# Cross-attention values straight from block-transposed probabilities, on sixteen 32x32 tiles

## The chip, the core and the metric

The kernel runs on one core of a Trainium2 chip. The metric is the time in microseconds of one execution on the device, lower is better. A core has five engines with instruction queues of their own that meet only at semaphores: TensorE (PE in the profile, its weight loads PEld), VectorE (DVE), ScalarE (ACT), GpSimd (POOL) and SyncE (SP), which here only issues DMAs. SBUF and PSUM have 128 partitions; PSUM has eight banks.

## The reference

```python
# x: (32, 512, 640) f32, ctx: (32, 77, 1024) f32; 20 heads of 32
q = heads(x @ to_q_w)
k, v = heads(ctx[:, :77] @ to_k_w), heads(ctx[:, :77] @ to_v_w)
s = einsum('bhqd,bhkd->bhqk', q, k) / sqrt(32)
h_txt = einsum('bhqk,bhkd->bhqd', softmax(s), v)
# the object, others and ip branches read ctx[:, 77:], which has no rows, and add nothing
out = merge(h_txt) @ to_out_w + to_out_b + x
```

Arithmetic is of fp32 accuracy.

## The kernel before

The program is one list of instructions per engine, in the order in which the Python code emits them (a manual schedule); what follows is therefore also the order in which each engine works.

**Keys and values of the context, once.** All 32 x 77 context rows are multiplied with the key and value weights in groups of 512 rows. Both results go to DRAM: `k_dram` with 128 channels on partitions, `v_dram` with a row for each context row. To keep fp32 accuracy, an operand of a large product is split into a high and a low part (type fp32r), and a product is three matmuls, high x high, high x low and low x high (`PAIRS`). A matmul on plain fp32 operands (scores and values) appears in the trace as two records, each with its own weight load.

**Slots.** The rest is 160 slots, `slot(n)`, with n = 5b + j: batch b (512 rows of x), and j one of five groups of four heads (128 channels). `HPC` is 4 heads, `NQ` 4 blocks of 128 query rows, `NC_` 5. A slot emits, for TensorE:

- `scores(n)`: 16 matmuls, 4 query blocks by 4 heads. Each uses one strip of 32 rows of the array (a head has 32 channels), so four heads go to four strips, with 128 query columns as weights and 77 keys as moving data. The four heads have a PSUM bank each (tag `sc`).
- `values(n - 3)`: 4 matmuls, one per head, over 80 rows (77 keys and padding, `KPAD`) and 512 query columns, on four strips of 32 columns. Result `pa`, one bank.
- `piece(b, i)`: part of the output projection of an earlier batch (`po`, `project`), two pieces per slot, 24 matmuls together. `STEPS` and `CUTS` say which.
- `queries(n + 1)`: 15 matmuls, the queries of the next slot (`pq`).

Beside it: `maxima(n)` on VectorE (negative row maxima of the scores), `exps(n, i)` on ScalarE (16 exponentials with row sums, head by head), `sums` and `normalize` (a reciprocal on VectorE, a multiplication on GpSimd, into `pn`, 80 columns per head), `high_a` and `low_a` (the split of `pa`, ScalarE copy and VectorE subtraction), `copy_q` (`pq` to `qt`), `transpose_x` and `split_x` (the x of the next batch, transposed by 32x32 blocks on VectorE, split on ScalarE and GpSimd), `add_bias` on GpSimd, and `finish`, which adds residual and bias to a finished half row block and sends the output.

**The way through DRAM.** The probabilities have queries on partitions, the values need keys there. `transpose_p(n - 1)` transposes 32x32 blocks on VectorE into `z`: partition 32a + i of a block of 32 keys then holds key i for the 128 queries of four runs of 32 rows (one run from each query block). The four partition groups a thus hold the same keys for different queries. Four DMAs per slot write this to `pd` in DRAM so that rows are keys, and `load_p` reads it back one to two slots later as `raw`, 80 keys by 4 heads by 512 queries. With these hops, `LAG` is 3: the values of slot n - 3 stand behind the scores of slot n. Padding columns of `pn` are zero, so what stands in the padding rows of the value tile counts for nothing.

The first slots only fill the pipeline, with no projection in them (`filling`), and the last context values are computed in slots 0 and 1 (`beside`). `end()` works off the last values and the last batch's projection.

Of the kernel before, what the change touches and what calls it, by code (L numbers as in the profile page):

```python
# [29 lines left out]
KPAD = 80  # L30
NBLK = HPC * KPAD // Q

# [5 lines left out]
def kernel(  # L38
# [185 lines left out]
    def load_x(b, quarters=range(4)):  # L224

        if b not in xss:
            xss[b] = xpool[0].tile([P, S // Q, C // 4], F32, tag="xs", name="xs")
# [9 lines left out]
    def split_x(b, c, high=nc.scalar.copy, low=nc.gpsimd):  # L237

        xt = xpool[0].tile([P, 2, S], FPR, tag="xt", name="xt", bufs=7)
# [12 lines left out]
    for _ in range(12):  # L252
        nc.tensor.matmul(warm, zero[:, :P], zero, start=True, stop=True)
# [110 lines left out]
    main = ctx.enter_context(tc.tile_pool(name="main", bufs=1, reuse_waits="tile"))  # L364
    ps = ctx.enter_context(tc.tile_pool(name="ps", bufs=1, space=PSUM, reuse_waits="tile"))
    psv = tc.alloc_tile_pool(name="psv", bufs=3, space=PSUM, side="right", reuse_waits="tile")
    late = []

    raws, ats, pds, sms, pqs, pas, xrs, pos, scs, nms, rss = ({} for _ in range(11))
# [4 lines left out]
    vbs = [main.tile([KPAD, NC_, HPC, HD], F32, name=f"vb{n}") for n in range(2)]  # L374
# [6 lines left out]
    z = main.tile([P, NBLK, NQ, Q], F32, name="z")  # L381
# [3 lines left out]
    def load_values(b):  # L385
        nc.sync.dma_start(vbs[b % 2], v_dram[b * NKEY : b * NKEY + KPAD])

# [16 lines left out]
    def scores(n):  # L404
        b, j = divmod(n, NC_)
        scs[n] = [ps.tile([P, NQ, P], F32, tag="sc", name="sc", bufs=4) for _ in range(HPC)]
# [33 lines left out]
    def sums(n):  # L440
        rss[n] = main.tile([P, NQ * HPC], F32, tag="rs", name="rs", bufs=2)
        nc.vector.reciprocal(rss[n], sms.pop(n))  # L442

    def normalize(n):
        rs = rss.pop(n)
        pf = pnb[n % 2][:, :, :NKEY]
        nc.gpsimd.tensor_tensor(  # L447
            pf, pf, rs.unsqueeze(2).to_broadcast([P, NQ * HPC, NKEY]), ALU.mult
        )

    def transpose_p(n):

        pn = pnb[n % 2]
# [4 lines left out]
        pd = dram.tile([NBLK * Q, S], F32, tag="pd", name="pd", bufs=6)  # L458
        rows = pd.rearrange("(b i) q -> i b q", i=Q)
        for a in range(4):  # L460
            nc.sync.dma_start(  # L461
                rows[:, :, a * P : (a + 1) * P],
                z[a * Q : (a + 1) * Q].rearrange("p b t j -> p b (t j)"),
            )
        pds[n] = pd

    def load_p(n):
        pd = pds.pop(n)
        raw = late[0].tile([KPAD, HPC, S], F32, tag="raw", name="raw", bufs=2)
        nc.sync.dma_start(raw, pd.rearrange("(h k) q -> k h q", h=HPC))  # L470
        raws[n] = raw

    def values(n):
        b, j = divmod(n, NC_)
        raw, vb = raws.pop(n), vbs[b % 2][:, j]
        pas[n] = late[1].tile([P, S], F32, tag="pa", name="pa", bufs=1)
        for i in range(HPC):
            nc.tensor.matmul(  # L478
                pas[n][i * HD : (i + 1) * HD, :],
                vb[:, i, :],  # L480
                raw[:, i, :],
                start=True,
                stop=True,
                tile_position=(0, i * HD),
            )

    def high_a(n):
        if n >= N - NC_ + 1:
            at = xpool[0].tile([P, 2, S], FPR, tag="xt", name="at", bufs=7)
        else:  # L490
            at = late[0].tile([P, 2, S], FPR, tag="at", name="at", bufs=8)
        nc.scalar.copy(at[:, 0, :], pas[n])  # L492
        ats[n] = at

    def low_a(n):
        at = ats[n]
        nc.vector.tensor_tensor(  # L497
            at[:, 1, :], pas.pop(n), at[:, 0, :].bitcast(F32), ALU.subtract
        )

    def load_residual(b, t, xr=None):
        if xr is None:
            xr = late[0].tile([P, C], F32, tag="xr", name="xr", bufs=4)
# [21 lines left out]
    STEPS = [(0, h, j) for h in range(2) for j in range(4)] + [(0, 0, 4), (0, 1, 4)]  # L525
    STEPS += [(t, h, j) for t in range(1, NQ) for h in range(2) for j in range(NC_)]
    CUTS = (0, 4, 8, 10, 16, 20, 24, 28, 32, 36, 40)
# [25 lines left out]
    LAG = 3  # L553

    takes = {n + LAG: n for n in range(N)}

    PIECES = {2: (1, 0), 3: (1, 2), 4: (1, 4), 0: (2, 6), 1: (2, 8)}
    RESIDUAL = {1: (1, 0), 2: (1, 1), 3: (1, 2), 4: (1, 3)}  # L560
    BIAS = {2: (1, 0), 3: (1, 1), 4: (1, 2), 0: (2, 3)}
    TRANSPOSE_X = {0: ((0,), (1,)), 1: ((2,), (3,))}
    SPLIT_X = {2: (0, 1), 3: (2, 3, 4)}
# [3 lines left out]

    def take(m):
        values(m)
        high_a(m)  # L570
        low_a(m)

    def slot(n, beside=()):
# [4 lines left out]
        xsplits = SPLIT_X.get(j, ()) if more and n > LATE else ()  # L578
        turns = TRANSPOSE_X.get(j, ((), ())) if more and b else ((), ())
        if b == 1 and j < 2:  # L580
            turns = (((), ()), ((0, 1), (2, 3)))[j]
        taken = takes.get(n)
        filling = not has_out
# [11 lines left out]
        if j == 1:  # L595
            load_values(b)
        if n == NC_:
            load_x(b + 1, (2, 3))
        if j == 4 and b and b + 2 < B:
            load_x(b + 2, (0, 1))  # L600
# [4 lines left out]
        if has_out:  # L605
            piece(bo_, first)
        for i in range(2):
            exps(n, i)
        if n:
            transpose_p(n - 1)  # L610
        finish()
        if j == 4 and b + 2 < B:
            load_x(b + 2, (0, 1) if not b else (2, 3))
        for i in turns[0]:
# [7 lines left out]
        if filling and ahead:  # L622
            copy_q(n + 1, nc.vector.tensor_copy)
        for i in range(2, HPC):
            exps(n, i)
        sums(n)
# [5 lines left out]
        if has_out:  # L632
            piece(bo_, first + 1)
        if taken is not None:
            low_a(taken)
        for c in xsplits:
            split_x(b + 1, c)
        for i in turns[1]:
            transpose_x(b + 1, i)
        finish()  # L640

    def end():
# [3 lines left out]
        load_p(N - 2)  # L646
        add_bias(last - 1, 3)
        piece(last - 1, 6)
        finish()
        transpose_p(N - 1)  # L650
        load_p(N - 1)
        load_residual(last, 0)
        load_residual(last, 1)
        piece(last - 1, 7)
        finish()
        take(N - 3)
# [3 lines left out]
        load_residual(last, 2)  # L660

        def begin(i, j0, j1):
            t, h = divmod(i, 2)
            if j0 == 0:
                if i < 4:
                    pos[last, t, h] = ps.tile([P, S], F32, tag="sc", name="po", bufs=4)
                elif i == 4:
                    pos[last, t, h] = ps.tile([P, S], F32, tag="pq", name="po", bufs=1)
# [100 lines left out]
```

## Time and profile before

| | us |
|---|---|
| median of 3 runs | 1806.47 (1802.81 to 1807.61) |
| the profiled execution, its own time | 1809.79 |
| its span (first to last instruction) | 1808.0 |
| slot 0 begins (scores) | 264.61 |
| slot 8, the first of the steady ones, begins | 345.17 |
| slot 159, the last, begins | 1770.00 |

Mean granted TensorE clock 0.987 of full speed. The DMA engines move 389 MB, 215 GB/s on average, and are busy for 0.91 of the steady part.

How to read the rows that follow. A row of the timeline has the start in the span, the length from the first start to the last end (us), engine, line, operation, output <- inputs, shapes and a count; in brackets, how long the engine had been idle and what ended that. `32*128` behind the names of a TensorE row is the part of the array in use, rows by columns. Rows of costly groups have busy time and mean ns of one, then idle time before them. Rows of one line's instructions have a count and the shortest, median and longest duration in ns. The rows of a stretch have its length, each engine's busy time with instruction counts, the granted clock, the DMA engines' busy share and GB/s. Rows of waits have total us, times, longest. Durations of matmuls and loads include pipeline latency: they overlap, so what counts is from start to start.

### The profile page before, as it was taken

The numbers are of one execution on the slowest core, as the hardware profiler recorded it, in microseconds if no ns is written. First come the engines' busy times: TensorE is split into PE (matmuls) and PEld (weight loads), VectorE is DVE, ScalarE is ACT, GpSimd is POOL, SyncE is SP. The second block draws the span as 40 slices with busy tenths as digits, with TensorE's granted clock in tenths as the row PEclk, the third lists the DMA queues.
The fourth block names the chain that finished last, engine by engine and source line by source line (L and its number), as shares of the span: only waits on it lengthen the run. The fifth ranks groups of instructions, "written<-read, shape, count | busy, mean of one in ns | idle before, by whom it ended". The sixth has DMA issues, their size and how long they took to land.

```text
span 1808.0 us, 39341 instructions
## 1 busy us (share of the span) xinstructions
PE 1763.3 (98%) x13852; PEld 1440.0 (80%) x13852; DVE 933.3 (52%) x1651; ACT 1108.9 (61%) x5698; POOL 789.7 (44%) x502
## 2 busy tenths in 40 slices
PE   8999998899999999999999999999999999999999
PEld 7888896678878888877788777888788888877787
DVE  5233134555555555555555555555555555545553
ACT  3132035666767777767677776677676777666662
POOL 0000034444445555545555545545555555535453
PEclk9999999999999999999999999999999999999999
DMA  9746465899999999998999999998899999898987
GB/s 186 149 94 174 105 168 138 211 231 235 232 232 239 232 243 235 240 235 219 237 232 237 228 230 237 230 233 230 229 234 230 229 240 237 229 224 219 236 207 202
DMA packets 465173, 389.12 MB, mean 215 GB/s; under 512 B 91280, under 2 KB 372368, under 8 KB 464976
## 3 DMA queue, kind: packets, MB, share of 16 engines
q1 hardware_dynamic: 462384, 379.49, 84.5%
q0 software_dynamic: 2496, 6.97, 1.3%
q8 instruction: 109, 1.79, 0.4%
q14 instruction: 88, 0.72, 0.1%
q10 hardware_dynamic: 96, 0.16, 0.0%
HBM read 223.82 MB, written 162.70 MB: 214 GB/s over the span
## 4 chain that ended last, share of the span: by engine, by line
PE 63%; DMA 17%; ACT 6%; POOL 6%; SPq 4%; DVE 2%; issue 2%; POOLq 0%; DVEq 0%; ACTq 0%
PE po L515 20%; PE pq L393 17%; PE pk L177 7%; PE pv L177 7%; DMA raw<-pd 6%; DMA pd<-z 6%; ACT pn L432 6%; PE sc L410 5%; PE pa L478 5%; POOL xt L243 4%; DMA xs<-in_x_dram 4%; SPq L461 2%; POOL pn L447 1%; SPq L231 1%; DVE xs L235 1%
## 5 line engine op out<-in xcount | busy, mean ns | idle before, releaser
L432 ACT ACTIVATE pn<-sc,nm 128x77 f32<-128x77 f32 x2560 | 787.4, 361 | 400.2 <-DVE nm L422 379.6
L515 PEld LDWEIGHTS po<-wo_s,at 128*128 128x128 f32 x3840 | 582.7, 190 | 143.8 <-issue 132.1
L447 POOL TENSOR_TENSOR pn<-pn,rs 128x1232 f32<-128x1232 f32 x160 | 364.0, 2275 | 665.1 <-DVE rs L442 659.9
L515 PE MATMUL po<-wo_s,at 128*128 128x320 f32 x3840 | 636.8, 316 | 0.0
L432 ACT ACTIVATION_READ_ACCUMULATOR pn<-sc,nm 128x1 f32 x2560 | 618.7, 242 | 0.0
L393 PE MATMUL pq<-xt,wq_s 128*128 128x512 f32 x2400 | 582.8, 395 | 0.0
L393 PEld LDWEIGHTS pq<-xt,wq_s 128*128 128x128 f32 x2400 | 450.1, 190 | 92.8 <-issue 4.9
L422 DVE TENSOR_REDUCE nm<-sc 128x4 f32<-128x308 f32 x640 | 261.0, 469 | 202.2 <-PE sc L410 202.1
L454 DVE STREAM_TRANSPOSE z<-pn 128x1280 f32<-128x1280 f32 x160 | 241.1, 1507 | 97.8 <-DMA pd<-z 92.3
L508 POOL TENSOR_TENSOR xr<-xr,bias 128x640 f32<-128x640 f32 x128 | 200.8, 1569 | 94.2 <-DMA xr<-in_x_dram 85.9
L243 POOL TENSOR_TENSOR xt<-xs,xt 128x512 fp32r<-128x512 f32 x160 | 200.0, 1274 | 35.6 <-ACT xt L242 35.6
L478 PE MATMUL pa<-raw,vb 80*32 80x512 f32 x1280 | 173.4, 613 | 27.6 <-DMA raw<-pd 19.6
L410 PEld LDWEIGHTS sc<-kb,qt 32*128 32x128 f32 x5120 | 157.5, 186 | 41.0 <-issue 35.1
L410 PE MATMUL sc<-kb,qt 32*128 32x77 f32 x5120 | 181.0, 277 | 8.7 <-DVE rs L442 5.8
L544 DVE TENSOR_TENSOR xr<-po,xr 128x320 f32<-128x320 f32 x256 | 117.5, 469 | 79.4 <-PE po L515 75.7
L235 DVE STREAM_TRANSPOSE xs<-xs 128x640 f32<-128x640 f32 x128 | 105.8, 832 | 74.2 <-DMA xs<-in_x_dram 74.2
L442 DVE RECIPROCAL rs<-sm 128x16 f32<-128x16 f32 x160 | 38.8, 243 | 196.3 <-ACT pn L432 196.3
L177 PE MATMUL pk<-ct,wk_s 128*128 128x512 f32 (+1 forms) x600 | 136.0, 387 | 3.1 <-ACT wk_s L89 3.1
L402 ACT COPY qt<-pq 128x512 f32<-128x512 f32 x153 | 93.3, 610 | 72.5 <-PE pq L393 72.1
L177 PE MATMUL pv<-ct,wv_s 128*128 128x512 f32 (+1 forms) x600 | 133.9, 381 | 0.0
L177 PEld LDWEIGHTS pk<-ct,wk_s 128*128 128x128 f32 x600 | 114.2, 191 | 23.2 <-ACT wk_s L89 3.6
L497 DVE TENSOR_TENSOR at<-pa,at 128x512 fp32r<-128x512 f32 x160 | 108.6, 679 | 37.2 <-ACT at L492 37.1
(31 smaller groups left out, 536.7 us busy)
## 6 DMA issues: line engine op xcount, KB each, us to landing
pd<-z SPq DMA_DIRECT2D x640, 160.0 KB, 5.4
raw<-pd SPq DMA_DIRECT2D x160, 640.0 KB, 5.5
xs<-in_x_dram SPq DMA_DIRECT2D x128, 320.0 KB, 6.0
xr<-in_x_dram SPq DMA_DIRECT2D x128, 320.0 KB, 5.7
out_dram<-xr SPq DMA_DIRECT2D x127, 320.0 KB, 3.9
vb<-v_dram SPq DMA_DIRECT2D x32, 200.0 KB, 6.0
kb<-k_dram SPq DMA_DIRECT2D x32, 192.5 KB, 7.3
cs<-in_ctx_dram SPq DMA_DIRECT2D x12, 512.0 KB, 9.4
```

Of the source, the lines that this page charges most:

```text
L177: nc.tensor.matmul(held[j][:, :gn], w[:, k, a, :], cts[g, k][:, c, :gn], start=(k == 0 and n == 0), stop=(k == NK - 1 and n == 2),)
L235: nc.vector.transpose(part, part)
L243: low.tensor_tensor(parts[1], src, parts[0].bitcast(F32), ALU.subtract)
L393: nc.tensor.matmul(pqs[n], wq_s[:, k, a, j * P : (j + 1) * P], xts[b, k][:, c, :], start=(k == 0 and m == 0), stop=(k == NC_ - 1 and m == 2),)
L410: nc.tensor.matmul(sc[:, t, :NKEY], qts[n % 2][r, t * P : (t + 1) * P], kbs[b % 2][r, j, :], start=True, stop=True, tile_position=(i * HD, 0),
L422: nc.vector.tensor_reduce(nms[n][:, i], sc[:, :, :NKEY], AX.X, ALU.max, negate=True)
L432: nc.scalar.activation(pnb[n % 2][:, at, :NKEY], sc[:, t, :NKEY], AF.Exp, bias=nms[n][:, i, t : t + 1], accum_out=sms[n][:, at : at + 1],)
L447: nc.gpsimd.tensor_tensor(pf, pf, rs.unsqueeze(2).to_broadcast([P, NQ * HPC, NKEY]), ALU.mult)
L454: nc.vector.transpose(z.rearrange("p b t j -> p t b j"), pn.rearrange("p (t h) k -> p t (h k)", t=NQ).rearrange("p t (b i) -> p t b i", i=Q),)
L478: nc.tensor.matmul(pas[n][i * HD : (i + 1) * HD, :], vb[:, i, :], raw[:, i, :], start=True, stop=True, tile_position=(0, i * HD),)
L508: nc.gpsimd.tensor_tensor(xrs[b, t], xrs[b, t], bias, ALU.add)
L515: nc.tensor.matmul(pos[b, t, h][:, :HALF], ats[b * NC_ + j][:, a, t * P : (t + 1) * P], wos[0][:, j, c, h * HALF : (h + 1) * HALF], start= ...
```

## The change

The values take `z` directly as moving data. The partition groups a and the four heads i give sixteen tiles of 32 rows by 32 columns. For each block of 32 keys (`KBLK` = 3, keys padded to 96) sixteen matmuls of 128 columns follow on sixteen different tiles; the three blocks accumulate in PSUM, one bank per a. `pd`, `raw` and their DMAs go; the value tile `vb` is loaded four times, once per partition group. The values of slot n - 1 now stand late in slot n, behind the queries and the first piece, and use banks of the scores' tag, which has five and not four. `z` and `vb` are doubled (the second copies live in a pool that opens after slot 1).

Beside this: the evacuation works on four banks (four copies, four subtractions), the reciprocal moves into `normalize`, `transpose_p(n - 1)` stands directly behind the maxima, all exponentials stand together, the first piece of a slot has 2 steps (of three matmuls) and the second 6, projections of a batch begin at j = 1, x is double buffered and loaded by quarters, residual tiles are 3, and 22 matmuls on zeros warm the array at the start where there were 12.

```diff
-KPAD = 80
+KPAD = 96
 NBLK = HPC * KPAD // Q
+KBLK = KPAD // Q
...
-    for _ in range(12):
+    for _ in range(22):
         nc.tensor.matmul(warm, zero[:, :P], zero, start=True, stop=True)
...
-    def load_values(b):
-        nc.sync.dma_start(vbs[b % 2], v_dram[b * NKEY : b * NKEY + KPAD])
+    def load_values(b, parts=range(4)):
+        src = v_dram[b * NKEY : b * NKEY + KPAD].rearrange("(c i) j h d -> i c (j h d)", i=Q)
+        for a in parts:
+            dst = vbs[b % 2][a * Q : (a + 1) * Q].rearrange("i c j h d -> i c (j h d)")
+            nc.sync.dma_start(dst, src)
...
     def transpose_p(n):
-        pn = pnb[n % 2]
+        pn, z = pnb[n % 2], zs[n % 2]
...
-        pd = dram.tile([NBLK * Q, S], F32, tag="pd", name="pd", bufs=6)
-        rows = pd.rearrange("(b i) q -> i b q", i=Q)
-        for a in range(4):
-            nc.sync.dma_start(
-                rows[:, :, a * P : (a + 1) * P],
-                z[a * Q : (a + 1) * Q].rearrange("p b t j -> p b (t j)"),
-            )
-        pds[n] = pd
-
-    def load_p(n):
-        pd = pds.pop(n)
-        raw = late[0].tile([KPAD, HPC, S], F32, tag="raw", name="raw", bufs=2)
-        nc.sync.dma_start(raw, pd.rearrange("(h k) q -> k h q", h=HPC))
-        raws[n] = raw
-
     def values(n):
         b, j = divmod(n, NC_)
-        raw, vb = raws.pop(n), vbs[b % 2][:, j]
-        pas[n] = late[1].tile([P, S], F32, tag="pa", name="pa", bufs=1)
-        for i in range(HPC):
-            nc.tensor.matmul(
-                pas[n][i * HD : (i + 1) * HD, :],
-                vb[:, i, :],
-                raw[:, i, :],
-                start=True,
-                stop=True,
-                tile_position=(0, i * HD),
-            )
+        z, vb = zs[n % 2], vbs[b % 2]
+        pas[n] = [ps.tile([P, S], F32, tag="sc", name="pa", bufs=5)[:, :P] for _ in range(4)]
+        for c in range(KBLK):
+            for a, pa in enumerate(pas[n]):
+                r = slice(a * Q, (a + 1) * Q)
+                for i in range(HPC):
+                    nc.tensor.matmul(
+                        pa[i * HD : (i + 1) * HD, :],
+                        vb[r, c, j, i, :],
+                        z[r, i * KBLK + c].rearrange("p t j -> p (t j)"),
+                        start=(c == 0),
+                        stop=(c == KBLK - 1),
+                        tile_position=(a * Q, i * HD),
+                    )
 
     def high_a(n):
...
-        nc.scalar.copy(at[:, 0, :], pas[n])
+        for a, pa in enumerate(pas[n]):
+            nc.scalar.copy(at[:, 0, a * P : (a + 1) * P], pa)
         ats[n] = at
...
-    CUTS = (0, 4, 8, 10, 16, 20, 24, 28, 32, 36, 40)
+    CUTS = (0, 2, 8, 10, 16, 18, 24, 26, 32, 34, 40)
...
     def slot(n, beside=()):
...
         scores(n)
-        if taken is not None:
-            values(taken)
         maxima(n)
-        if n - LAG + 1 in pds and n > LATE:
-            load_p(n - LAG + 1)
+        if n:
+            transpose_p(n - 1)
...
         if ahead:
             queries(n + 1)
+        if has_out:
+            piece(bo_, first)
+            if not ahead:
+                piece(bo_, first + 1)
+        finish()
+        if ahead and not has_out:
+            copy_q(n + 1, nc.vector.tensor_copy)
+        for i in range(HPC):
+            exps(n, i)
+        if n:
+            values(n - 1)
...
         normalize(n)
-        if taken is not None:
-            high_a(taken)
+        if n:
+            high_a(n - 1)
+            low_a(n - 1)
+        for i in turns:
+            transpose_x(b + 1, i)
         if has_out and ahead:
             copy_q(n + 1)
-        if has_out:
             piece(bo_, first + 1)
-        if taken is not None:
-            low_a(taken)
         for c in xsplits:
             split_x(b + 1, c)
-        for i in turns[1]:
-            transpose_x(b + 1, i)
         finish()
```

More of the change, by code (lines that the diff above doesn't have):

```diff
@@ L373 @@
     kbs = [main.tile([P, NC_, NKEY], F32, name=f"kb{n}") for n in range(2)]
-    vbs = [main.tile([KPAD, NC_, HPC, HD], F32, name=f"vb{n}") for n in range(2)]
+    vbs = [main.tile([P, KBLK, NC_, HPC, HD], F32, name="vb0")]
     pnb = []
@@ L405, in scores @@
         b, j = divmod(n, NC_)
-        scs[n] = [ps.tile([P, NQ, P], F32, tag="sc", name="sc", bufs=4) for _ in range(HPC)]
+        scs[n] = [ps.tile([P, NQ, P], F32, tag="sc", name="sc", bufs=5) for _ in range(HPC)]
         for t in range(NQ):
@@ L552 @@
     LATE = 2
[L553 to L563, printed above, removed]
+    PIECES = {1: (1, 0), 2: (1, 2), 3: (1, 4), 4: (1, 6), 0: (2, 8)}
+    RESIDUAL = {0: (1, 0), 1: (1, 1), 2: (1, 2), 3: (1, 3)}
+    BIAS = {1: (1, 0), 2: (1, 1), 3: (1, 2), 4: (1, 3)}
+    TRANSPOSE_X = {0: (0, 1), 1: (2, 3)}
+    SPLIT_X = {1: (0,), 2: (1, 2), 3: (3, 4)}
     WO = {1: (0, 1, 2), 2: (3,), 3: (4,)}
     wos = []
[L568 to L571, printed above, removed]
     def slot(n, beside=()):
@@ L594, in slot @@
             load_keys(b + 1)
[L595 to L600, printed above, removed]
+        if j in (2, 3) and more:
+            load_values(b + 1, (2 * j - 4, 2 * j - 3))
+        if b + 2 < B:
+            quarters = {4: (0, 1), 5: (2, 3)}.get(n, ()) if n <= NC_ else (j - 1,) if j else ()
+            if quarters:
+                load_x(2 if n <= NC_ else b + 2, quarters)
         if j in RESIDUAL and b >= RESIDUAL[j][0]:
@@ L645, in end @@
         last = B - 1
[L646 to L649, printed above, removed]
         transpose_p(N - 1)
[L651 to L656, printed above, removed]
+        for t in range(2):
+            load_residual(last, t)
         piece(last - 1, 8)
@@ L724 @@
     )
-    load_p(0)
+    zs.append(late[0].tile([P, NBLK, NQ, Q], F32, name="z1"))
+    vbs.append(late[0].tile([P, KBLK, NC_, HPC, HD], F32, name="vb1"))
     for n in range(LATE, N):
```

120 lines of the change are left out of this document (46 added, 74 removed).

## The prediction

> **What bounds the kernel now.** I read the page first, then one slot of the steady part in order of time, and at the end the slots that are longer than the rest.
>
> ```profile
> span 1808.0 us, 39341 instructions
> PE 1763.3 (98%) x13852; PEld 1440.0 (80%) x13852; DVE 933.3 (52%) x1651; ACT 1108.9 (61%) x5698; POOL 789.7 (44%) x502
> pd<-z SPq DMA_DIRECT2D x640, 160.0 KB, 5.4
> raw<-pd SPq DMA_DIRECT2D x160, 640.0 KB, 5.5
> ```
>
> TensorE is busy for 98% of the span. The way through DRAM that the change removes (640 writes of pd, 160 reads back as raw) can give time only where TensorE waits for it. A busy matmul row hides pipelining, so I take one slot (one batch and one group of four heads) from the starts of its weight loads:
>
> ```profile
> 1002.70 0.98 PEld L410 LDWEIGHTS sc<-kb,qt 32*128 32x128 f32 x32 [0.19 <-issue]
> 1003.76 0.16 PEld L478 LDWEIGHTS pa<-raw,vb 80*32 80x32 f32 x8
> 1004.76 0.88 PEld L515 LDWEIGHTS po<-wo_s,at 128*128 128x128 f32 x6 [0.84 <-issue]
> 1005.59 3.31 PEld L393 LDWEIGHTS pq<-xt,wq_s 128*128 128x128 f32 x15
> 1008.94 2.75 PEld L515 LDWEIGHTS po<-wo_s,at 128*128 128x128 f32 x18
> 1011.89 0.20 PEld L410 LDWEIGHTS sc<-kb,qt 32*128 32x128 f32 x4 [0.19 <-issue]
> ```
>
> The blocks follow one another with no gap: scores 1.06, values 1.00, projection 0.83, queries 3.35, projection 2.95, together 9.19 us. No other engine ends a wait here that TensorE feels. Whole stretches against that:
>
> ```profile
> 345.17:1770.00 1424.83, 1402.43 (x11931) 1139.29 (x11930) 791.30 (x1416) 991.19 (x5282) 715.34 (x422) 0.99 0.91 232
> L478 PEldq EVENT_SEMAPHORE  x151: 51/51/682, 345.5 to 1761.1; - x151
> PE pa L478 <- DMA raw<-pd: 16.1, 15, 3.1
> 1030.27 0.98 PEld L410 LDWEIGHTS sc<-kb,qt 32*128 32x128 f32 x32 [0.19 <-issue]
> 1032.18 0.19 PEld L478 LDWEIGHTS pa<-raw,vb 80*32 80x32 f32 x8 [0.92 <-PE sc L410]
> ```
>
> The first row is a stretch with its length and the busy time of PE, PEld, DVE, ACT, POOL; the second counts the values blocks in it: 151 slots. 151 x 9.19 = 1387.7, so 37.1 us of 1424.8 lie over the undisturbed slot. The last two rows show where: the values, due 1.06 us after the scores, begin 1.91 us after them, because raw has not landed. So the prize in the steady part is at most 37 us, 2% of the span. Against it stands what the new values cost on TensorE, 160 times. Everything else is small.
>
> **The values on sixteen tiles.** Before, a values block is 4 matmuls (8 records, as each fp32 matmul runs in two passes) over 512 columns, on four column strips. After, it is 3 x 4 x 4 = 48 matmuls, 96 records, each 32 rows, 32 columns of weights and 128 columns of moving data, ordered so that sixteen different tiles follow one another. What a record costs depends on how many tiles work at once, and the trace shows four at once in two ways:
>
> ```profile
> L410 PEld LDWEIGHTS sc<-kb,qt x4: 181/181/181, 1002.7 to 1002.7; 32*128 32x128 f32 x4
> L410 PE MATMUL sc<-kb,qt x4: 329/329/329, 1002.7 to 1002.7; 32*128 32x77 f32 x4
> L478 PEld LDWEIGHTS pa<-raw,vb x4: 106/106/106, 1003.8 to 1003.8; 80*32 80x32 f32 x4
> L478 PE MATMUL pa<-raw,vb x8: 592/605/617, 1003.8 to 1004.2; 80*32 80x512 f32 x8
> 1002.46 0.31 PE L515 MATMUL po<-wo_s,at 128*128 128x320 f32 x1
> 1003.76 1.07 PE L478 MATMUL pa<-raw,vb 80*32 80x512 f32 x8
> 1005.74 3.59 PE L393 MATMUL pq<-xt,wq_s 128*128 128x512 f32 x15
> 1009.16 2.80 PE L515 MATMUL po<-wo_s,at 128*128 128x320 f32 x18
> ```
>
> The first two rows (count, durations in ns) are all of the scores that starts between 1002.69 and 1002.74, the third all loads of the values between 1003.75 and 1003.785: four tiles begin within 35 ns, so one follows the next by at most 35/4 = 9 ns; I use 7. The fourth row is the values' whole block. Row strips (scores) and column strips (values) both do it; both at once is nowhere in the trace.
>
> Times of one record, from these rows. A load of 128 columns shows 181 ns and one of 32 columns 106, so 96 columns are 75 to 80 ns and 32 columns about 27 (128: 107). In the values the last of 8 matmuls starts 1.07 - 0.59 = 0.48 us after the first; less 20 ns of stagger and 27 of load, 512 columns take 0.43 us a pass, and 128 take 0.107. Scores: the 32 loads end 0.98 after the first begins, the last lasts 0.18, so eight groups of four start (0.98 - 0.18 - 0.02)/7 = 0.11 us apart, which is the load of 128 columns plus 5 ns. A tile of the new values has the same step for the other reason: 107 of streaming plus 5, 112 ns, its next load (27) hidden beneath. It does six of them (three key blocks, two passes).
>
> All sixteen at once: load 0.03, five steps 0.56, stagger 15 x 0.007 = 0.10, last pass 0.11, drain 0.10 (what the old block's 1.00 has left after 0.03 + 0.43 + 0.02 + 0.43). Sum 0.89 us against 1.00. But the tile shape now changes four times a slot and not three, because queries and projection stand between scores and values. One more change costs the drain ahead (from the last projection at 1002.46 to the scores' load is 0.24, against a pitch of (2.75 - 0.18)/17 = 0.15 inside the block: 0.09) and a first load of 128 columns that nothing hides (0.11): 0.20. **Per slot: -1.00 + 0.89 + 0.20 = +0.09, about +0.10; over 151 slots +15 us.**
>
> Can the instructions come that fast? 192 of them (a load and a matmul per record) would have to in some 0.7 us:
>
> ```profile
> 297.61 1.01 PEld L410 LDWEIGHTS sc<-kb,qt 32*128 32x128 f32 x32 [1.28 <-ACT pn L432]
> L478 PEldq EVENT_SEMAPHORE  x1: 51/51/51, 297.9 to 297.9; - x1
> ```
>
> Here, in an early slot, the scores had to wait, so little stood ready; 0.3 us later the sequencer has gone through all 64 score instructions and stands at the values' wait. That is at most 4.7 ns each, or 0.9 us for 192: between free and 0.2 us a slot. I take free, since the queue holds work already while it waits on the 21 matmuls ahead, and keep 0.2 x 159 = 32 us as an upper end.
>
> [...]
>
> **The waits.** The stalls over 9.19 go: values now need only z, transposed on VectorE a slot after its probabilities, and no DMA: -37 us. What is late next:
>
> ```profile
> 1003.85 1.64 DVE L422 TENSOR_REDUCE nm<-sc 128x4 f32<-128x308 f32 x4 [2.41 <-PE sc L410]
> 1004.42 0.33 ACT L432 ACTIVATE pn<-sc,nm 128x77 f32<-128x77 f32 x1 [1.69 <-DVE nm L422]
> 1008.93 0.41 ACT L432 ACTIVATE pn<-sc,nm 128x77 f32<-128x77 f32 x1
> 1009.23 0.68 ACT L492 CAST at<-pa 128x512 fp32r<-128x512 f32 x1
> 1009.70 0.70 ACT L402 COPY qt<-pq 128x512 f32<-128x512 f32 x1
> L454 DVE STREAM_TRANSPOSE z<-pn 128x1280 f32<-128x1280 f32 x160 | 241.1, 1507 | 97.8 <-DMA pd<-z 92.3
> L497 DVE TENSOR_TENSOR at<-pa,at 128x512 fp32r<-128x512 f32 x160 | 108.6, 679 | 37.2 <-ACT at L492 37.1
> L544 DVE TENSOR_TENSOR xr<-po,xr 128x320 f32<-128x320 f32 x256 | 117.5, 469 | 79.4 <-PE po L515 75.7
> L235 DVE STREAM_TRANSPOSE xs<-xs 128x640 f32<-128x640 f32 x128 | 105.8, 832 | 74.2 <-DMA xs<-in_x_dram 74.2
> ```
>
> Counted from the scores' start. Transposed probabilities: maxima end at 2.8, the transpose grows to 1507 x 96/80 = 1808 ns and ends at 4.6; values start at 1.06 + 0.11 + 3.42 (queries, 1005.74 to 1009.16) + 0.99 (six projections: 5 x 0.15 + 0.24) = 5.58. Covered by 1 us. PSUM banks: the values take four of the five score banks, the last freed by the third group of exponentials. Those start at 1.72, 0.30 apart; the twelfth ends at 1.72 + 11 x 0.30 + 0.41 = 5.43. Covered by 0.1 only. Scores of the next slot: they need banks that the values' evacuation frees, and qt, whose copy stands behind that evacuation on ScalarE. Evacuation starts at 6.53; four copies of 128 columns (between an exp of 77, 0.36, and the 0.68 of 512: 0.40) end by 8.1, the four subtractions (estimate 0.28 each from 679 for 512) by 8.4, qt by 8.8. Next scores at 9.29. Covered by 0.5; if not, each 0.1 us costs 15.
>
> VectorE closes the thin margin. With j = 0 it still has two x transposes (1.66) and up to two output additions (0.94) behind the subtractions: 8.4 + 2.6 = 11.0, where the next maxima could start at 9.29 + 1.15 = 10.44. Exponentials are then up to 0.6 late and the values of the next slot up to 0.5; in the other slots it fits. 31 batches x 0.3 = **+10 us** (0 to 45, the upper end being 0.3 in every slot). The SP queue loses 800 issues and gains 96 for four copies of the values; x loads are spread by quarters: no cost, as nothing in the slot waits for them within a slot.
>
> **Start, filling, end.**
>
> ```profile
> 8.00:15.20 7.20, 6.04 (x15) 4.59 (x15) 5.29 (x9) 3.48 (x8) 0.00 (x0) 0.53 1.04 200
> 17.49 3.56 PE L177 MATMUL pk<-ct,wk_s 128*128 128x512 f32 x15
> 264.61:345.17 80.56, 66.64 (x514) 51.49 (x513) 37.48 (x67) 45.95 (x268) 36.15 (x31) 0.92 0.69 160
> 290.37 1.01 PEld L410 LDWEIGHTS sc<-kb,qt 32*128 32x128 f32 x32 [1.70 <-issue]
> 322.78 1.01 PEld L410 LDWEIGHTS sc<-kb,qt 32*128 32x128 f32 x32 [1.92 <-ACT at L492]
> 1770.00:1808.00 38.00, 34.22 (x257) 29.77 (x256) 13.41 (x25) 7.25 (x36) 11.76 (x8) 0.99 0.67 193
> ```
>
> The first real matmuls run at a granted clock of 0.53 and take about 6 us, where the next fifteen take 3.4. Ten more warming matmuls may keep the clock up: -2 (0 to -2.7, if the loads let it). Slots 0 to 7 last 80.6. After, slot 1 holds a values block (+0.9); slots 2 to 5 are bound by their chain, 7.2 before (290.37 to 297.61), about 8.3 with the evacuation in it, 33 together where they had 32.4 with stalls (290.37 to 322.78); slots 6 and 7 are full ones of 9.3 where they took 22.4 (to 345.17), and the projections start a slot earlier: -2 (-8 to +5). The end keeps 168 projections of 192 and two values blocks of four, but waits about 1 us for the last probabilities: -4 (-6 to 0).
>
> **Sum**: +15 - 37 + 10 - 2 - 2 - 4 = -20 us. The profiled execution took 1809.8 (span 1808.0), 3.3 above the median of 1806.5; the same difference off the median gives **1786 us**.
>
> **The rivals.** *Four at a time* (slower). If sixteen tiles in both directions do not overlap more than four do, because a strip takes one tile at a time (0.10) or because a record costs the scores' average of 28 ns (0.08), the block is 24 groups x 0.112 + 0.2 = 2.9 us, 2.0 more than forecast: x 159 = +318, 2104 us. It decides against the change as soon as the block exceeds 0.89 + 20/159 = 1.02 us. For it: no row shows both directions at once. Against it: either direction alone runs four within 35 ns, a second pass of one tile waiting while other tiles go ahead, so tiles are queued apart; loads and streams of one strip overlap. Together 0.18. *Feed or thin margins* (about the same to slower): the sequencer's 0.2 us a slot, or a wait of 0.3 us for banks or qt in every slot, each 1786 + 32 to 38, about 1821, with part of either 1800 to 1850. For it: the margin of 0.1 us. Against it: it needs every slot late, where the rows give one in five. Chance 0.20. *The forecast*, 1760 to 1801: 0.62. Its lower end has no new waits (-10) and the extra change of shape free (-15).
>
> About 0.3% (5 us) is what can be told from no change. Faster: the forecast, 0.62. Same: 0.05 of the second rival. Slower: 0.15 of it and the first, 0.33. The range takes in the second rival, 1760 to 1850, and leaves out the first.
>
> **What would show it.** Right: loads of pa x96 spanning about 0.7 us, the projection's load 0.9 after their first, scores 9.2 to 9.4 us apart with no long slot in five, no wait of pa for a DMA. Wrong: a values block of 2.5 us or more; or pa waiting for pn or ScalarE, scores for at or qt, in most slots.

## The result, and the profile after

| | before | after |
|---|---|---|
| median, us | 1806.05 (1802.81 to 1807.61, 4 runs) | 1900.28 (1897.9 to 1910.52, 4 runs) |
| the profiled execution | 1809.79 | 1910.52 |

The ratio after to before is 1.0537, 95% interval 1.0502 to 1.0573: slower by 94 us where 20 us less was forecast. The profiled execution is the longest of the four; the others are 10 us shorter. The first lines of the page after, and its DMA queue that brings instructions (packets, MB, share of 16 engines' span):

```profile
span 1908.7 us, 67569 instructions
PE 1876.6 (98%) x27942; PEld 1600.2 (84%) x27942; DVE 1008.7 (53%) x2130; ACT 1145.7 (60%) x6179; POOL 790.1 (41%) x502
q8 instruction: 219, 3.59, 0.8%
```

TensorE is busy for the same 98%, of a longer span, and has twice the instructions (27942 loads and as many matmuls, where there were 13852 of each). One undisturbed slot, from the timeline of weight loads:

```profile
1007.03 0.98 PEld L419 LDWEIGHTS sc<-kb,qt 32*128 32x128 f32 x32 [0.19 <-issue]
1008.09 3.27 PEld L402 LDWEIGHTS pq<-xt,wq_s 128*128 128x128 f32 x15
1011.40 0.99 PEld L513 LDWEIGHTS po<-wo_s,at 128*128 128x128 f32 x6
1012.58 1.22 PEld L473 LDWEIGHTS pa<-z,vb 32*32 32x32 f32 x96 [0.19 <-issue]
1014.00 2.64 PEld L513 LDWEIGHTS po<-wo_s,at 128*128 128x128 f32 x18 [0.20 <-issue]
1016.83 0.20 PEld L419 LDWEIGHTS sc<-kb,qt 32*128 32x128 f32 x4 [0.19 <-issue]
```

From start to start: scores 1.06, queries 3.31, first projection 1.18, values 1.42 (1.41 in most slots), second projection 2.83, together 9.80 us where it was 9.19. Queries and projections take 7.32 where they took 7.13, so the fourth change of tile shape costs 0.19, as forecast (0.20). The values take 1.41 against a forecast of 0.89 and 1.00 before. The first two rows of the next view are the values' matmuls that started by 1012.84, then all of them; the third is VectorE's transpose that makes their moving data:

```profile
1012.59 0.50 PE L473 MATMUL pa<-z,vb 32*32 32x128 f32 x32
1012.59 1.48 PE L473 MATMUL pa<-z,vb 32*32 32x128 f32 x96
L460 DVE STREAM_TRANSPOSE z<-pn 128x1536 f32<-128x1536 f32 x160 | 282.7, 1767 | 5.9 <-POOL pn L453 5.9
```

32 of the 96 matmuls start within 0.25 us, across sixteen tiles in both directions; then it slows down. The stretches (length, busy time and count of PE, PEld, DVE, ACT, POOL, granted clock, DMA share, GB/s): slots 8 to 158, one slot in them, slots 0 to 7, the end, the first matmuls:

```profile
345.26:1874.25 1528.99, 1509.49 (x25218) 1287.69 (x25217) 862.19 (x1868) 1024.49 (x5734) 714.39 (x422) 0.99 0.40 101
384.57:399.89 15.32, 12.80 (x168) 10.59 (x167) 5.19 (x13) 7.65 (x40) 6.09 (x4) 0.78 0.23 63
262.33:345.26 82.93, 77.60 (x1169) 65.26 (x1168) 42.83 (x92) 49.86 (x293) 39.04 (x33) 0.94 0.47 118
1874.25:1908.70 34.45, 29.72 (x393) 27.87 (x392) 12.50 (x27) 6.57 (x40) 9.65 (x6) 1.00 0.30 104
8.00:15.20 7.20, 6.07 (x26) 4.54 (x25) 5.38 (x10) 3.80 (x8) 0.00 (x0) 1.00 1.22 204
```

The steady stretch is 104.2 us longer: 151 x (9.80 - 9.19) = 92.1, and 49.2 over the undisturbed slot (1528.99 - 151 x 9.80) where 37.1 were before. With the start of slot 0 (264.61 to 262.33, -2.3), slots 0 to 7 (+2.4) and the end (-3.6) that makes the +100.7 between the two profiled executions.

Of the 49.2 us, 45 are of two kinds; the remaining 4 lie in slots of 9.85 and 9.87 us. The first kind was forecast: in the slot after j = 0 the values wait for the third head's exponentials, which free their bank, and the slot takes 0.36 us longer (a slot from the timeline, then the row of the waits in 345.26 to 1874.25):

```profile
435.02 0.28 PEld L473 LDWEIGHTS pa<-z,vb 32*32 32x32 f32 x24 [0.19 <-issue]
435.53 1.02 PEld L473 LDWEIGHTS pa<-z,vb 32*32 32x32 f32 x72 [0.22 <-ACT pn L441]
...
PEld pa L473 <- ACT pn L441: 7.3, 28, 0.5
```

27 slots of 10.15 for 9.80 make about 10 us. The second kind was not: seven slots take 13.8 to 15.7 us and one 11.8, together 35 us over 9.80. The slot of the second stretch above:

```profile
384.57 0.75 PEld L419 LDWEIGHTS sc<-kb,qt 32*128 32x128 f32 x23 [0.19 <-issue]
387.99 0.71 PEld L419 LDWEIGHTS sc<-kb,qt 32*128 32x128 f32 x9 [2.66 <-issue]
388.84 5.57 PEld L402 LDWEIGHTS pq<-xt,wq_s 128*128 128x128 f32 x15
```

TensorE stops in the middle of the scores for 2.66 us, and nothing ends the idle time but "issue": no semaphore, no engine, no DMA that the program waits for. The queries behind it then take 5.57 us for 3.27, at a granted clock that is 0.78 over the slot. What it lacked was instructions: of the packets in the instruction queue (times from the trace's records; a packet is 16 KB), one starts at 372.10 and the next at 385.46, while the usual distance is 7.7 us. TensorE goes on at 387.99, 1.42 us after that packet has landed. Between them SyncE, released by an output, had issued these (timeline of SyncE):

```profile
375.39 0.34 SPq L547 DMA_DIRECT2D out_dram<-xr  x1
375.83 0.38 SPq L232 DMA_DIRECT2D xs<-in_x_dram  x1
376.30 0.51 SPq L502 DMA_DIRECT2D xr<-in_x_dram  x1
376.87 0.93 SPq L395 DMA_DIRECT2D vb<-v_dram  x2
377.85 0.42 SPq L232 DMA_DIRECT2D xs<-in_x_dram  x1
378.37 0.44 SPq L502 DMA_DIRECT2D xr<-in_x_dram  x1
```

That is 2.1 MB within 3.4 us. The packet starts when this burst is over: the next two rows are the stretch before it and one that begins within the stop.

```profile
378.00:385.30 7.30, 7.30 (x150) 6.48 (x148) 4.19 (x9) 5.35 (x30) 2.60 (x2) 1.00 1.05 227
387.00:393.80 6.80, 5.81 (x21) 4.61 (x22) 3.32 (x5) 4.49 (x30) 0.73 (x1) 0.50 0.01 4
```

The DMA engines are full (1.05) up to the packet and idle behind it. From within the stop on the granted clock is 0.50 for 6.8 us, in which the queries take most of their 5.57 us. The page of before has 109 packets in that queue for 27704 TensorE instructions, the page of after 219 for 55884: 254 and 255 instructions a packet. Twice the instructions need a packet twice as often (7.7 us apart, 15 before). A late packet alone does not stop TensorE: in the steady stretch 18 packets come 13.1 to 14.4 us after the last, all in or behind such a burst (the DMA engines at 1.04 to 1.09 in the 7 us ahead of each), and only eight of them go with a stop, in the eight long slots. What the eight share is the place: TensorE stands each time at the same count of its records, 193 over a multiple of 256 (6081, 9409 and 17857 at the first three, loads, matmuls and semaphore waits counted), and goes on 1.3 to 1.6 us after the packet has landed. At the other ten it had not come to that place when the packet arrived: it came there 1.3 to 3.5 us after the landing.

### The profile page after: what moved, and what is told of

It is laid out like the page before. It is cut to its first block, busy times and chain, and to the rows that moved or that the text cites. A ratio compares the mean times of both kernels' runs of the same rounds, so it can differ in the third digit from the quotient of the medians.

```text
span 1908.7 us, 67569 instructions
## 1 busy us (share of the span) xinstructions
PE 1876.6 (98%) x27942; PEld 1600.2 (84%) x27942; DVE 1008.7 (53%) x2130; ACT 1145.7 (60%) x6179; POOL 790.1 (41%) x502
## 4 chain that ended last, share of the span: by engine, by line
PE 97%; issue 1%; DVE 1%; ACT 0%; DMA 0%; POOL 0%; SPq 0%; DVEq 0%; ACTq 0%
PE po L513 31%; PE pq L402 31%; PE pa L473 12%; PE sc L419 9%; PE pv L178 7%; PE pk L178 7%; ACT pn L441 0%; DMA wraw<-in_L_xattn_to_k_w_dram 0%; DVE z L460 0%; POOL pn L453 0%; DVE nm L431 0%; POOL v_dram L217 0%; DVE at L495 0%; SPq L146 0%; DVE xr L541 0%
## 5 line engine op out<-in xcount | busy, mean ns | idle before, releaser
L402 PE MATMUL pq<-xt,wq_s 128*128 128x512 f32 x1680 | 439.9, 410 | 4.8 <-issue 4.8
L402 PEld LDWEIGHTS pq<-xt,wq_s 128*128 128x128 f32 x1680 | 312.1, 193 | 76.6 <-issue 5.1
L460 DVE STREAM_TRANSPOSE z<-pn 128x1536 f32<-128x1536 f32 x160 | 282.7, 1767 | 5.9 <-POOL pn L453 5.9
L473 PE MATMUL pa<-z,vb 32*32 32x128 f32 x15360 | 247.2, 278 | 2.1 <-DVE z L460 1.6
L473 PEld LDWEIGHTS pa<-z,vb 32*32 32x32 f32 x15360 | 181.9, 103 | 55.9 <-issue 33.1
L506 POOL TENSOR_TENSOR xr<-xr,bias 128x640 f32<-128x640 f32 x128 | 200.8, 1569 | 10.7 <-DVE xr L541 5.7
L402 PE MATMUL pq<-xu,wq_s 128*128 128x512 f32 x720 | 183.0, 398 | 0.0
L488 ACT CAST at<-pa 128x128 fp32r<-128x128 f32 x640 | 126.3, 296 | 90.9 <-PE po L513 41.7
L495 DVE TENSOR_TENSOR at<-pa,at 128x128 fp32r<-128x128 f32 x640 | 141.2, 283 | 69.8 <-ACT at L488 63.8
L402 PEld LDWEIGHTS pq<-xu,wq_s 128*128 128x128 f32 x720 | 136.9, 190 | 33.2
L247 POOL TENSOR_TENSOR xt<-xs,xt 128x512 fp32r<-128x512 f32 x112 | 141.7, 1279 | 54.9 <-ACT xt L246 50.0
```

The costliest lines, as they stand in the source:

```text
L247: low.tensor_tensor(parts[1], src, parts[0].bitcast(F32), ALU.subtract)
L402: nc.tensor.matmul(pqs[n], wq_s[:, k, a, j * P : (j + 1) * P], xts[b, k][:, c, :], start=(k == 0 and m == 0), stop=(k == NC_ - 1 and m == 2),)
L460: nc.vector.transpose(z.rearrange("p b t j -> p t b j"), pn.rearrange("p (t h) k -> p t (h k)", t=NQ).rearrange("p t (b i) -> p t b i", i=Q),)
L473: nc.tensor.matmul(pa[i * HD : (i + 1) * HD, :], vb[r, c, j, i, :], z[r, i * KBLK + c].rearrange("p t j -> p (t j)"), start=(c == 0), stop ...
L495: nc.vector.tensor_tensor(at[:, 1, cols], pa, at[:, 0, cols].bitcast(F32), ALU.subtract)
L506: nc.gpsimd.tensor_tensor(xrs[b, t], xrs[b, t], bias, ALU.add)
```

## The experiments

My theories after the result: for the block, **feed** (instructions arrive too slowly for sixteen tiles) against **streaming** or **tiles** (a tile or a column costs more than thought); for the long slots, **fetch** (a packet of instructions behind a burst of loads) against another wait; for the comparison as a whole, **load** (part of what changed is only the finer loading of x). Experiments that ran together share their runs of before, whose medians were 1808.7 to 1812.5.

### A quarter of the columns

Each values matmul streams 32 columns and not 128, and the result is repeated four times in the evacuation, whose work stays:

```diff
-pa[i * HD : (i + 1) * HD, :],
+pa[i * HD : (i + 1) * HD, :Q],
 vb[r, c, j, i, :],
-z[r, i * KBLK + c].rearrange("p t j -> p (t j)"),
+z[r, i * KBLK + c, 0],
...
```

> After, with a quarter of the moving columns: each of the 48 value matmuls streams 32 columns instead of 128 (only the first of four query blocks; its result is repeated for the others). The same 192 instructions and loads on TensorE per slot. Feed theory (beyond the 64 instructions that stand ready, TensorE gets a new one every 4.2 ns, and the first of them 0.3 us late): the values block, 1.41 us, loses only the streaming of the last pass and of the two first tiles of a round that wait for themselves, 3 x 0.08, so about 1.17, and the run takes 1855 to 1885. Streaming theory (sixteen tiles together share a path, so columns set the length): block 0.4 to 0.6, run about 1750.

Measured 1837.93 us (1832.19 to 1842.77), ratio to before 1.0159 (1.0124 to 1.0193). Its values in the timeline:

```profile
760.54 0.91 PEld L473 LDWEIGHTS pa<-z,vb 32*32 32x32 f32 x96 [0.19 <-issue]
761.49 2.64 PEld L517 LDWEIGHTS po<-wo_s,at 128*128 128x128 f32 x18
```

The block is 0.95 us, between the theories: a quarter of the streaming leaves 0.95, most of it the supply of 192 instructions (the steps below), and 0.46 of the 1.41 do hang on the columns. Most slots are 9.32 to 9.41 (9.69 behind j = 0); eight long ones remain (11.4 to 15.6 us), so those come with the count of instructions, which is the same, and not with the length of the block.

### One record per matmul

Upper halves of the fp32 words as bf16 operands: the same 48 matmuls with 48 records, of lower precision.

```diff
-vb[r, c, j, i, :],
-z[r, i * KBLK + c].rearrange("p t j -> p (t j)"),
+vb[r, c, j, i, :].bitcast(mybir.dt.bfloat16)[:, 1::2],
+z[r, i * KBLK + c].rearrange("p t j -> p (t j)").bitcast(mybir.dt.bfloat16)[:, 1::2],
```

> After, with the values' operands read as the upper halves of their fp32 words (bf16): one record per matmul, 48 records and 96 instructions instead of 192; precision is lower, all else is the same. Feed theory: the first 64 instructions, now two whole rounds of sixteen tiles, start without a gap between the rounds at about 7 ns a tile, and a gap comes only ahead of the third round; block about 0.7 us, run about 1786. Tile theory (a tile that is used again stalls what stands behind it): a gap ahead of the second round as well, block about 0.95, run about 1826.

Measured 1738.49 us (1736.42 to 1738.99), ratio 0.9608 (0.9583 to 0.9633).

```profile
722.65 0.47 PEld L473 LDWEIGHTS <-vb 32*32 32x32 bf16 x48 [0.19 <-issue]
723.19 2.64 PEld L513 LDWEIGHTS po<-wo_s,at 128*128 128x128 f32 x18
...
337.93:1701.84 1363.91, 1356.32 (x17970) 1168.33 (x17969) 849.99 (x1868) 1013.86 (x5735) 715.97 (x422) 1.00 0.45 113
```

The block is 0.54 us, below what either theory gave. The slot is 8.99 most often, and the stretch of 151 slots is only 6.4 us longer than 151 of them (1363.91 - 151 x 8.99). No slot is long, though packets of instructions come late here too (13 over 13 us after the last, one 17.1): the usual distance is 9.6 us, and each late one landed before TensorE had come to the place of the stops. How the matmuls of one block follow one another is worked out from the trace's records (ns from start to start, in order of time):

```
after, block at 395.643 us, 96 starts over 1218 ns
  7 7 6 7 7 6 7 7 6 7 7 6 7 7 6 | 34 | 6 7 7 6 7 7 6 7 7 6 7 7 6 7 7 | 85 109 | 8 17 16 17 17 16 17 17 14 2 15 2 ...
a quarter of the columns, 96 starts over 829 ns
  7 7 6 7 7 6 7 6 1 5 1 6 1 6 ... | 86 31 | 9 16 17 17 0 16 0 17 0 17 ...
one record, 48 starts over 379 ns
  4 3 3 4 3 3 4 3 3 4 3 3 4 3 3 | 20 | 4 3 3 3 6 1 6 2 4 ... | 131 | 8 8 9 8 8 9 8 8 9 8 8 9 8 8 9
```

In all three, 32 records start fast and then comes a pause. With two records to a matmul that is one round of the sixteen tiles, with one record two rounds: 64 instructions (32 loads, 32 matmuls) come ahead of the pause in all three runs, and I read them as what stands ready. From there, where nothing else holds it, a matmul follows each 16.7 ns with its four instructions and each 8.3 ns with two: 4.17 ns an instruction, with the full columns as with a quarter of them. The array itself is not the limit, as the first 32 records start faster (3.3 ns apart with one record). That is the feed, shown.

### Loads moved within the batch

The value tiles at j = 3 and 4 where they were at 2 and 3, x quarters at j = 0 to 3 where they were at 1 to 4:

```diff
-if j in (2, 3) and more:
-    load_values(b + 1, (2 * j - 4, 2 * j - 3))
+if j in (3, 4) and more:
+    load_values(b + 1, (2 * j - 6, 2 * j - 5))
-quarters = {4: (0, 1), 5: (2, 3)}.get(n, ()) if n <= NC_ else (j - 1,) if j else ()
+quarters = {4: (0, 1), 5: (2, 3)}.get(n, ()) if n <= NC_ else (0, 1) if n == 6 else (j,) if j < 4 else ()
```

> After, with the loads of SyncE spread: the value tiles at j = 3 and 4 instead of 2 and 3, quarters of x at j = 0 to 3 instead of 1 to 4. Fetch theory (the 7 long slots of 13.8 to 15.7 us stop inside the scores because a 16 KB packet of TensorE's instructions comes 5 us late, behind 2 MB that SyncE has issued at once after its long wait for an output): no gap of over 12 us between instruction packets in the steady part, no long slots, run about 1865. Rival (twice the instructions are too many for the fetch as such): long slots stay, run about 1900.

Measured 1884.13 us (1883.64 to 1886.49), ratio 1.042 (1.0387 to 1.0452). Slots over 11 us go from eight (11.8 to 15.7) to three (11.1, 12.0 and 12.7), time over the undisturbed slot from 49 to 21 us, the longest distance of two instruction packets from 14.4 to 12.3 us. The direction is the fetch theory's, the size short of it (no long slot and 1865 were expected), as some late packets remained. So a second arrangement has all four value tiles at j = 4, where no x quarter is, and the x quarter of j = 2 behind the first `finish()`:

```diff
-if j in (2, 3) and more:
-    load_values(b + 1, (2 * j - 4, 2 * j - 3))
+if j == 4 and more:
+    load_values(b + 1)
...
-if quarters:
+if quarters and j != 2:
...
 finish()
+if j == 2 and b and b + 2 < B:
+    load_x(b + 2, (2,))
```

> After, with SyncE's loads spread further: all four value tiles at j = 4, quarters of x at j = 0 to 3, that of j = 2 behind the first output of its slot, so that between two outputs never more than 1.3 MB are issued (2.1 before the change of this run, 1.8 in spread). Fetch theory: the two long slots left in spread go as well, steady excess over 9.80 about 14 us (the bank wait, and slots of 9.87), run about 1872. Rival (spread gained by chance of alignment): 1885 to 1900.

Measured 1875.41 us (1875.12 to 1875.54), ratio 1.0346 (1.0305 to 1.0387). No long slot, 14.1 us over the undisturbed slot, longest distance of packets 10.7 us. The program's instructions are the same in number and kind; only when the loads start differs. Long slots, longest distance and time fall together, 25 us below after. With the common place of the stops that is the fetch, shown. What is left over the undisturbed slot is about the bank wait.

### Which tile begins a round

In after's blocks the 17th matmul (tile 0 again) holds all behind it for 109 ns. In this version round c begins with row strip c:

```diff
-for a, pa in enumerate(pas[n]):
+for a, pa in [((u + c) % 4, pas[n][(u + c) % 4]) for u in range(4)]:
```

> After, with each round of sixteen tiles begun one row strip further (round c begins with the tile in row strip c). First-of-round theory (whichever tile comes first after the ready instructions are used waits for its own first pass and holds all behind it): the 109 ns steps stay at the 17th matmul and at the third round, block 1.41, run 1885 to 1910. Rival (it is tile 0 that is special, or the distance of sixteen between two uses of a tile): the steps move or go, block 1.2 to 1.3 or longer than 1.5.

Measured 1902.19 us (1894.45 to 1906.7), ratio 1.049 (1.0447 to 1.0533); block 1.41 to 1.42. The steps of 85 and 109 stay where they are, so it is not tile 0's own pass that is waited for but whatever stands first in the second round. The third round has no step of 109 in either kernel, unlike expected: its longest is 45 in after and 36 here, and the sum of the block's steps is the same (1217 ns). Why one first matmul holds fifteen others on free tiles stays open.

### The kernel before with the finer loads

x double buffered and loaded by quarters at j = 1 to 4, all else as before:

```diff
-xss[b] = xpool[0].tile([P, S // Q, C // 4], F32, tag="xs", name="xs")
+xss[b] = xpool[0].tile([P, S // Q, C // 4], F32, tag="xs", name="xs", bufs=2)
...
-if j == 4 and b and b + 2 < B:
-    load_x(b + 2, (0, 1))
...
+quarters = {4: (0, 1), 5: (2, 3)}.get(n, ()) if n <= NC_ else (j - 1,) if j else ()
```

> Before, with x in two buffers and loaded by quarters over j = 1 to 4 (as in the changed kernel) instead of in halves around j = 4. Load theory (the values wait for raw in the slots with j = 4 because two halves of x are in the queues ahead of pd and raw): the 37 us over the undisturbed 9.19 us slot mostly go, run about 1775. Rival (the way through DRAM is too slow in itself): 1806.

Measured 1860.25 us (1853.92 to 1863.02), ratio 1.0278 (1.0245 to 1.0311). The steady stretch and a row of its waits:

```profile
348.24:1822.04 1473.80, 1415.79 (x11931) 1141.44 (x11930) 781.62 (x1416) 994.37 (x5282) 716.41 (x422) 0.99 0.90 224
...
PE pa L478 <- DMA raw<-pd: 33.7, 31, 3.0
```

The load theory fell: the finer loads do not help the old kernel, they cost it 49 us in the stretch (1473.80 against 1424.83), with twice the waits for raw (31 for 33.7 us, where 15 took 16.1). Its DMA engines were at 0.91 and are at 0.90. The x loads now stand beside the way through DRAM in four slots of five, and the long slots move with them: the seven over 11 us before have j = 1, and 14 of the 15 here have j = 3.

### The kernel before with one record per matmul

The same bf16 halves in the old values (again lower precision), to see which way is better when a matmul is one record:

```diff
-vb[:, i, :],
-raw[:, i, :],
+vb[:, i, :].bitcast(mybir.dt.bfloat16)[:, 1::2],
+raw[:, i, :].bitcast(mybir.dt.bfloat16)[:, 1::2],
```

> Before, with the values' operands read as the upper halves of their fp32 words (bf16), as in one_pass: 4 records of 512 columns instead of 8. Precision is lower, all else is the same. Block theory (the way through DRAM costs only its stalls): the values block falls from 1.00 to about 0.36, the undisturbed slot to 8.55, the stalls stay at 37, the run takes about 1704, less than one_pass with 1738, so the way through DRAM would be the better one at equal precision too. Rival (the DMA engines, busy for 0.91 of the steady part, cannot deliver raw in shorter slots): more and longer waits for raw, 1740 to 1800.

Measured 1802.76 us (1795.44 to 1805.82), ratio 0.9941 (0.9922 to 0.996). The values of one slot with the projection behind them, then a slot in which they waited, its stretch and a row of its waits:

```profile
924.16 0.10 PEld L478 LDWEIGHTS <-vb 80*32 80x32 bf16 x4
924.51 1.76 PEld L515 LDWEIGHTS po<-wo_s,at 128*128 128x128 f32 x12 [0.24 <-issue]
...
932.12 0.98 PEld L410 LDWEIGHTS sc<-kb,qt 32*128 32x128 f32 x32 [0.19 <-issue]
935.67 0.13 PEld L478 LDWEIGHTS <-vb 80*32 80x32 bf16 x4 [2.57 <-DVE xr L544]
935.70 0.42 PE L478 MATMUL pa<-raw,vb 80*32 80x512 bf16 x4 [2.45 <-DMA raw<-pd]
...
347.65:1756.49 1408.84, 1328.34 (x11326) 1147.95 (x11325) 787.99 (x1416) 982.65 (x5282) 716.41 (x422) 0.98 0.92 234
PE pa L478 <- DMA raw<-pd: 48.1, 23, 3.1
```

The values fall from 1.00 to 0.35 us and the undisturbed slot from 9.19 to 8.56, 95 us over 151 slots, but the stretch gets only 16 us shorter: 116 us over the undisturbed slots stand where 37 did. For the loads at 935.67 the profile names VectorE's xr, for their matmuls 0.03 us later raw. So the block theory fell, and the rival's waits are there, at a time just over its range: 52 slots take longer than 8.66 us, and the 19 over 11 us all have j = 1. That the DMA engines, at 0.92, have no more to give is argued and not shown; what is shown is that the path that the change removes cost more in the shorter slot (116 us at 8.56, 37 at 9.19).

### Both edits

One record per matmul in the new kernel, and the loads as in the second arrangement.

> After with both edits, one pass per value matmul (upper halves of the fp32 words, lower precision) and the spread loads of spread2. Fetch theory: one_pass has no long slot (its packets of instructions last 9.6 us and not 7.7), so spreading has nothing left to take: 1730 to 1740, the same as one_pass with 1738. Rival (the spread loads also shorten ordinary slots): under 1728.

Measured 1737.0 us (1735.89 to 1739.4), ratio 0.9585 (0.9566 to 0.9603). It beats both kernels, at lower precision in the values. Without long slots there was nothing left for the second edit to take, so it adds nothing (1738.49 without it).

## Why the prediction was wrong, point by point

**Can the instructions come that fast? I took free.** This is the step that failed. The row that I had (64 score instructions in at most 0.3 us) gave at most 4.7 ns each and 0.9 us for the block; measured are 4.17, though that row covers only as many instructions as turned out to stand ready, so the agreement may be luck. But I let the queue's stock cover the block, and priced the rest at 0.2 us at most. The stock that the runs show is 64 instructions of 192. The 0.2 was a difference of two totals, 0.9 of feed against 0.7 of streaming, as if they ran side by side from the start. Here they ran one behind the other: the first round is streamed from stock in 0.23 us, then 0.19 us (the steps of 85 and 109 ns) pass until the 17th matmul's first pass has gone through, then the rest of the second round takes 0.34 us and the third 0.45, where the supply alone (30 and 32 records at 8.3 ns) would take 0.25 and 0.27. First start to last start is 1.22 us, where the sum had five steps of 0.112 and 0.10 of stagger, 0.66; the whole block is 1.41 for 0.89. 151 x 0.52 = 79 us of the error in the steady stretch, which is 116 us (+104 for -12). The quarter of the columns bounds the parts: 0.95 with little streaming, 0.46 that come only with the full columns. Of the 0.46, the steps of the two runs place 0.08 in the first 32 records, 0.08 in the 17th matmul's own pass, 0.06 in the rest of the second round, 0.17 in the third round and 0.07 behind the last start. Why the third round holds so much is open.

**The stalls go.** Right for the cause named: no wait of pa for a DMA is left, and the DMA share of the steady stretch falls from 0.91 to 0.40. Wrong in the sum: "what is late next" listed engines, banks and qt, and not the instructions themselves, whose number the change doubles. The stops for their packets cost 35 us, as much as the stalls that went (37). The second arrangement of the loads, with these stops gone and all else kept, is still at 1.035 of before, so the block decides and the fetch adds.

**Thin margins.** Right in place and size: the bank of the third group of exponentials, behind the slot with j = 0, 0.36 us in 27 slots, 10 us for 10. The cause is the one forecast too: in the slot at 429.42 the maxima start 1.70 us after the scores, behind x transposes and output additions on VectorE, where they start 1.15 after them in the slot at 1007.03. In the steady stretch scores never wait for qt or at, and the values start 5.55 us after the scores, forecast 5.58. The transpose takes 1767 ns for 1808.

**Start, filling, end.** -2.3 for -2 (the clock of the first matmuls is 1.00 where it was 0.53), +2.4 for -2 and within its bounds, -3.6 for -4. **The fourth change of tile shape**: 0.19 for 0.20.

**The rivals.** *Four at a time* is wrong: sixteen tiles start 7 ns apart while instructions stand ready (3 with one record). Behind that the pace of 16.7 ns a matmul, 8.3 a record, hangs on the instructions and not on the array. Over the whole block a record takes 12.8 ns on average (1218 ns for 95 steps), where the rival took the scores' 28 (0.11 us for four). Neither its block of 2.9 us nor its 2104 us came. *Feed or thin margins* named the mechanism, at 32 us and a chance of 0.20; the block's excess is 83 us over 160 slots, two and a half times that, and the fetch was not in it. The block from which the change loses, 1.02 us, fits the runs: 1.41 without any long slot loses 3.5%, 0.54 without any wins 4%, and 0.95, near the border, loses 1.6% with eight long slots.

## What to carry to other kernels

Count instructions as well as streaming: here the records of sixteen tiles started 6.7 ns apart while instructions stood ready, and the instructions behind the first 64 of 192 brought a record each 8.3 ns at best. So only what stood ready was fast, and the two times added up rather than hid one another (0.46 us for three quarters of the columns, where six passes of one tile lose about 6 x 0.08, an estimate from 0.107 us a pass). Twice the TensorE instructions also came in twice the packets (219 for 109), and all 18 late packets here stood in or behind a burst of loads, so bursts of loads then belong apart from one another: the second arrangement, with its loads apart, took 25 us less than after. Removing a transfer paid here where it was what the slot waited for: the same change lost 5% with two records per matmul and won 3 to 4% with one (1738.49 against 1802.76), where the old way had 116 us of waits.

## What was not expected of the hardware

- In the values' blocks of after, of a quarter of the columns and of one record, 64 TensorE instructions came ahead of the first pause, which I read as what stood ready; those behind followed at 4.17 ns each where nothing else held them, after a pause of 0.12 to 0.19 us.
- Sixteen tiles of 32 by 32 started 6.7 ns apart with two records per matmul, 3.3 ns with one, while instructions stood ready. With two, the first sixteen records last 292 ns and the next sixteen 267: I read them as first and second passes, a second pass starting behind the first passes of fifteen later matmuls, but the records do not name the tile.
- The first matmul of the second round held the fifteen behind it for 109 ns with two records and full columns and for 31 with a quarter of them; which tile is first made no difference (steps of 85 and 109 ns, block 1.41 to 1.42 us, with another tile first). Why is open.
- A packet of instructions that came 13.4 us after the last, behind a burst of loads, stopped TensorE for 2.66 us, and the granted clock was 0.50 for 6.8 us from within the stop on: a slot of 15.3 us for 9.8, of which less than half was the stop itself. Ten other packets of the run came as late and stopped nothing: TensorE came to the place of the stops 1.3 to 3.5 us after they had landed.
